# One pool of PSUM pairs for layer 0 and product 2, and block sums made inside the feature runs

## The chip, the cores and the metric

The kernel runs on one core of a Trainium2 chip. The core has TensorE (PE: matmuls, with its weight loads shown as PEld), VectorE (DVE), ScalarE (ACT), GpSimd (POOL) and SyncE (SP), whose queue starts most of the DMA transfers. Matmul results land in PSUM, which has eight banks of 512 fp32 values on each of 128 partitions; PE writes there, DVE and ACT read there. The metric is the device time of one execution in microseconds. Three executions of the kernel before gave 1660.17, 1660.75 and 1664.76 us, so its median is 1660.75.

## The reference, cut to what matters

The input is `x` (8 batches, 2048 nodes, 64 features) and an adjacency matrix `adj` (2048 x 2048). Four layers follow each other, each of the form `x = layernorm(x + layer(x))`, all in fp32.

```python
def _L0_gnn_ref(x, A, embedding, weight, bias):        # K = 3
    w = einsum('nd,dkio->nkio', embedding, weight)     # one weight matrix for every node
    b = einsum('nd,do->no', embedding, bias)
    As = [eye(N), A, 2.0 * (A @ A) - eye(N)]
    x_g = einsum('knm,bmc->bnkc', stack(As), x)
    return einsum('bnki,nkio->bno', x_g, w) + b
...
x = layernorm(x + L0(x, adj, embedding, weight, bias))
x = layernorm(x + L1(x, adj, net_params))      # z = relu((adj @ z) @ W), two times
x = layernorm(x + L2(x, adj, ...))             # x @ Wself + (adj @ x) @ Wneigh + bias
x = layernorm(x + L3(x, adj, adj, weight, bias))   # x, adj@x, adj@(adj@x) side by side, times weight, + bias
```

Each layer needs one or two products of `adj` with a 2048 x 512 matrix (8 batches of 64 features side by side). There are seven, one after another: the code's first stage makes product 0, and six calls of the function `product` make products 1 to 6. Layer 0 uses products 0 and 1, layer 1 uses 2 and 3, layer 2 uses 4, layer 3 uses 5 and 6.

## The kernel before

**A product of matrices with fewer multiplications.** `product` splits `adj` and the data into two by two quarters and uses seven products of quarters in place of eight (A11, S1, A12, S2, S4, S3, A22 in this order). Each of the seven is done by `inner`, which splits once more in the same manner: seven block products of 512 x 512, each one load of 1 MB of `adj` (or of sums of its blocks) and eight (in products 4 and 6, 32 smaller) matmul records on PE. `inner` first makes four block sums of its data, `t1` to `t4`, on DVE (`less`, L534). It then uses three PSUM banks a, b, c in the order `a+=`, `b+=`, `a+=`, `b+=`, `c+=`, `b+=`, `c+=` (L568 to L594). After the first block product ACT copies bank a to `p1` (L574), because the third accumulates onto it. In products 2 to 6 four of the seven inner products (`FORMED`) go instead through `fast_inner`, which splits twice more and uses seven banks after one another (L480 to L510); the sums of `adj` that it needs, the "forms", are made beforehand.

**Layer 0's feature step.** Whenever a block of product 1 (512 nodes x 2 batches, 16 blocks in all) is done, `hand_over` adds a job `feature0` to the pump. A job has four groups of nodes, and two halves of the embedding for each: a tile `y` of two PSUM banks, 12 matmul records. Of the first half (an odd tile) DVE takes eight readings (L1514, `xy += y * e`). Of the second half (an even tile) ACT takes eight (L1518, `s = y * e`), which POOL adds up in three steps (L1524) and onto `xy` (L1527). The job yields after each tile: these are its eight steps.

**The pump.** `Pump` holds jobs and, in `later`, normalizations that wait for a number of steps. `tick`, called at each step, counts these down; a normalization of a pair of blocks comes due three times: its square on ACT (L865), then the rest (the sum L872 and small steps on DVE, the root L881 on ACT, the scaling L893 on DVE), then its end. `run` works off whole jobs without the inner products between them. Beside them, after each step, it advances a list of side jobs at a given rate per step, and at its end it finishes them. Layer 0 has two runs: four jobs after S2 of product 1 (run 1, 32 steps, rate 1.25, side work: the forms of S1), and the other twelve at the start of product 2 (run 2, 96 steps, rate 0.97, side work: the forms of A12, S2 and S4). `make_forms` yields four times while its first tiles load and then once for each of 28 forms per quarter; 18 of the 28 are made by DVE and 10 by POOL (L289, L292), and each that is kept is stored by a transfer on SP's queue (L269).

**Order.** The framework schedules each engine's instructions at compile time, by when it thinks they are ready, and adds the semaphores. Instructions in `keep_in_program_order` stay behind everything written earlier for their engine: DVE's readings of `y`, the forms, POOL's adds, the first matmul of an odd `y` tile, the block sums of `inner` at the places in question, and the first seven loads of product 2. ACT's readings, `sq`, the root and the copy `p1` are not pinned.

**PSUM.** Before layer 0's second stage the banks belong to the pools `p_n` (`ps_n`) and `p_tn` (`ps_e`), four each. Then `p_mm` (two banks) serves the inner products, and `p_y` (three pairs, six banks) the `y` tiles. `to_late`, at the start of product 2, gives back `p_y` and allocates `p_mm2` (two banks, used in turn with `p_mm` from then on, see `bank`) and `p_z` (four banks).

**The run of the calls in `product`.** Product 1: A11, S1, A12, then a run of one job (a weight preparation), S2, run 1 (L788), S4, S3, A22. Product 2: run 2 (L697), then `to_late` and A11 (L744) with its block sums, S1 and the rest.

Of the kernel before, what the change touches and what calls it, by code (L numbers as in the profile page):

```python
# [9 lines left out]
F32 = mybir.dt.float32  # L10
AF = mybir.ActivationFunctionType
ALU = mybir.AluOpType
# [4 lines left out]
P = 128  # L17
EPS = 1e-5
GW = 512
# [38 lines left out]
class Pump:  # L58
# [32 lines left out]
                self.later.remove(job)  # L91

    def tick(self, idle=False):
        for job in list(self.later):

            job[0] -= 0.5 if idle and job[4] else 1
            if job[0] <= 0:
                job[0], job[4] = job[1], False
                if next(job[2], "done") == "done":
                    self.later.remove(job)  # L100

    def run(self, n=None, side=(), rate=1):

        side, owed = list(side), 0
        while self.jobs and n != 0:
            for _ in self.jobs[0]:
                self.tick()
                owed += rate
                while owed >= 1:
                    owed -= 1  # L110
                    if side and next(side[0], "done") == "done":
                        side.pop(0)
            self.jobs.pop(0)
            n = None if n is None else n - 1
        for job in side:
            for _ in job:
                pass
# [23 lines left out]
def kernel(  # L141
# [91 lines left out]

    loads = 0
    pieces = []
    banks = 0
    p_mm2 = None

    def load(q, s, forms=False):
        nonlocal loads  # L240
# [65 lines left out]
    def product(src, feature, between=None, rate=1, own=None, pin=False, runs=None, onto_slot=None, ends=False, fast=(), forms={}):  # L306
# [18 lines left out]
            return sums.tile([P, 4, GW], F32, tag="C", name="C", bufs=4)  # L325

        def bank(n):
            nonlocal banks
            banks += 1
            pool = p_mm if p_mm2 is None or banks % 2 else p_mm2  # L330
            return pool.tile([P, GW], F32, tag="mm", name=f"mm{n}")

        class InTile:

# [176 lines left out]
            if end is not None:  # L511
                end()

        def inner(q, b, finish, early=None, tail=None, next_sum=None, home=None, held=False):

            b11, b12, b21, b22 = (
                b[:, hm * TG : (hm + 1) * TG, ts(hc, 2 * F)] for hm in range(2) for hc in range(2)
            )  # L520

            places = [] if home is None else [tiled(home[:, k]) for k in range(4)]

            def new():
                if places:
                    return places.pop(0)
                return sums.tile([P, TG, 2 * F], F32, tag="t", name="t", bufs=TB)


            pin = tc.keep_in_program_order if places or pump.hold or held else lambda inst: inst  # L530

            def less(a, b):
                out = new()
                pin(nc.vector.tensor_tensor(out, a, b, ALU.subtract))  # L534
                return out

            t1 = less(b12, b11)
            t2 = less(b22, t1)
            t3 = less(b22, b12)
            t4 = less(b21, t2)  # L540
            if next_sum is not None and home is None:
                next_sum()

            def mul(ps, s, xb, start, stop=True):
                a = load(q, s)
                if onto_slot is not None:

                    for k in range(TG):
                        for m in range(TG):
                            if isinstance(ps, list):  # L550
                                to = ps[k // (TG - 1)][:, ts(k % (TG - 1), P)]
                                opens = k % (TG - 1) == 0
                            else:
                                to, opens = ps[:, ts(k, P)], k == 0
                            nc.tensor.matmul(  # L555
                                to, a[:, k, m, :], xb[:, m, :], start=(start and opens and m == 0),
                                stop=(m == TG - 1), skip_group_check=True,
                            )
                    pump.step(pump.rate)
                    return  # L560
                for m in range(TG):
                    nc.tensor.matmul(  # L562
                        ps, xb[:, m, :], a[:, :, m, :], start=(start and m == 0),
                        stop=(m == TG - 1), skip_group_check=True,
                    )
                pump.step(pump.rate)

            pa, pb = bank("a"), bank("b")  # L568
            mul(pa, 0, b11, True)
            if next_sum is not None and home is not None:  # L570

                next_sum()
            p1 = sums.tile([P, GW], F32, tag="p1", name="p1")
            nc.scalar.copy(p1, pa)  # L574
            if early is not None:
                early(2, p1)
            mul(pb, 5, t2, True)
            u2 = add(sums.tile([P, GW], F32, tag="u2", name="u2"), pb, p1)
            if early is not None:
                early(1, u2)  # L580
            mul(pa, 1, b21, False)
            finish(0, pa, None)
            mul(pb, 6, t3, False)
            u3 = add(sums.tile([P, GW], F32, tag="u3", name="u3"), pb, p1)
            if early is not None:
                early(3, u3)
            pc = bank("c")
            mul(pc, 4, t1, True)
            if tail is None:
                finish(3, pc, u3)  # L590
                mul(pb, 3, t4, False)
                finish(2, pb, p1)
                mul(pc, 7, b22, False)
                finish(1, pc, u2)  # L594
            else:
                parts = [p_z.tile([P, GW], F32, tag="z", name=f"mmd{h}") for h in range(2)]
                tail(pc, pb, parts, lambda: mul(pb, 3, t4, False), lambda: mul(parts, 7, b22, True))

        def fresh(c):
            def finish(blk, ps, plus):  # L600
                if plus is None:
                    nc.scalar.copy(c[:, blk, :], ps)
                else:
                    add(c[:, blk, :], ps, plus)
            return finish,

        def onto(c, base, give=None, then=None):

            def early(blk, plus):
                add(c[:, blk, :], base[:, blk, :], plus)  # L610
                if give is not None and onto_slot is not None:
                    add(tiled(c[:, blk, :]), place(*give, blk), tiled(c[:, blk, :]))

            def finish(blk, ps, plus):
                if give is not None and onto_slot is not None:
                    if plus is None:
                        add(place(*give, blk), place(*give, blk), tiled(base[:, blk, :]))
                    add(place(*give, blk), tiled(ps), place(*give, blk) if plus is None else tiled(c[:, blk, :]))
                else:
                    add(c[:, blk, :], ps, (base if plus is None else c)[:, blk, :])  # L620
                if give is not None:
                    hand_over(c, *give, blk)
                if then is not None:
                    then(blk)
            return finish, early
# [64 lines left out]
        give = onto_slot is not None  # L690
        waits = pump.hold and runs is None

        def side(q):
            return [make_forms(*forms[q])] if q in forms else []

        if waits:
            pump.run(None, side(A11), 0.97)  # L697
            pump.hold = False
        pump.pass_mark()

# [39 lines left out]
        if A11 in fast:  # L740
            next_sum()
            fast_inner(A11, b11, InTile(u), clear(u))
        else:
            inner(A11, b11, *fresh(u), home=home, next_sum=next_sum, held=waits)  # L744
        if pump.hold and not waits:
            pump.run()
            pump.hold = False
# [37 lines left out]
            fast_inner(S2, t2, InTile(u), None, join_all)  # L785
        else:
            inner(S2, t2, *onto(u, u, then=join))
        pump.run(runs.get(S2, 0), side(S2), 1.25)  # L788
        if S4 not in fast:
            inner(S4, b22, *onto(c, c, (0, 1)))  # L790
        elif give:
            fast_inner(S4, b22, InPlace(0, 1), spread(0, 1, c), hand_all(u, 0, 1))
        else:
            fast_inner(S4, b22, InTile(c), None, hand_all(c, 0, 1))
# [150 lines left out]
    if True:  # L945
# [487 lines left out]
            )  # L1433
            yield

        p_mm = ctx.enter_context(tc.tile_pool(name="p_mm", bufs=2, space=PSUM))
        if True:
            p_y = first.enter_context(tc.tile_pool(name="p_y", bufs=3, space=PSUM))
            l0y = first.enter_context(tc.tile_pool(name="l0y", bufs=1))

            def last_back():
# [93 lines left out]
    late = p_z = None  # L1535

    def to_late():
        nonlocal late, p_z, p_mm2, ring2, loads
        first.close()
        late = ctx.enter_context(tc.tile_pool(name="late", bufs=1))  # L1540
        ring2 = ctx.enter_context(tc.tile_pool(name="ring2", bufs=3))
        loads = 0
        p_mm2 = ctx.enter_context(tc.tile_pool(name="p_mm2", bufs=2, space=PSUM))
        p_z = ctx.enter_context(tc.tile_pool(name="p_z", bufs=4, space=PSUM))

    def pair_transposed(g, p, slot):
# [117 lines left out]
```

## Time and profile before

One execution was profiled. It took 1660.59 us; the span from its first to its last instruction is 1658.8 us.

| engine | busy, us | share of the span |
|---|---|---|
| PE | 1628.8 | 98% |
| PE weight loads | 1167.0 | 70% |
| DVE | 1128.8 | 68% |
| POOL | 572.1 | 34% |
| ACT | 308.6 | 19% |

The mean granted clock of PE is 0.996. Product 1 starts at 208.6 us, run 1 at 305.7, its S4 at 388.3, run 2 at 465.6, product 2's first matmul at 727.5.

How to read the lines below: in a list of groups or in the timeline a row names engine, line of the code, operation, output and inputs, and in brackets how long the engine sat idle before it and what ended that. A row of the waits reads "who <- for whom: total us, times, longest us". In the chain, a row is start, length and the work that held up the end. A row of a stretch (`392.00:401.00`) gives its length, the busy time and the number of instructions of PE, PEld, DVE, ACT and POOL, the granted clock of PE (1.00 is full), the share of the DMA engines and GB/s. Times are microseconds from the start of the span.

### The profile page before, as it was taken

What the parts mean: (1) busy time and instruction counts of PE and PEld (TensorE: products, weight loads), DVE (VectorE), ACT (ScalarE), POOL (GpSimd) and SP (SyncE); (2) the same over time, 40 slices, a digit from 0 to 9 for tenths busy, and PEclk for the clock granted to TensorE, in tenths of its full rate; (3) what the DMA queues carried; (4) which work ended last, traced back from release to release, by engine and by line L of the source; (5) the groups of instructions that cost most, each with busy time, mean ns of one, the idle gap of its engine ahead of it and who ended that gap; (6) DMA issues with size and microseconds to landing.
All of it is one profiled execution on the core that took longest, in us unless ns stands there. A gap on an engine that the chain in (4) does not pass through costs nothing.

```text
span 1658.8 us, 23256 instructions
## 1 busy us (share of the span) xinstructions
PE 1628.8 (98%) x8886; PEld 1167.0 (70%) x8886; DVE 1128.8 (68%) x1889; ACT 308.6 (19%) x870; POOL 572.1 (34%) x582
## 2 busy tenths in 40 slices
PE   9999999999999999989999999999999999999998
PEld 5998844444444444547875688579999688669998
DVE  5996795686458787755764378875689456644687
ACT  0210100243024344421111011221111012100111
POOL 1121100383037677763701451024522442025510
PEclk9999999999999999999999999999999999999999
DMA  8999999646843545369787877656888865678885
GB/s 312 358 389 375 347 334 323 232 149 238 304 159 117 201 137 185 105 234 345 274 288 259 286 279 254 227 211 236 292 295 298 293 247 199 251 249 282 305 308 176
DMA packets 101390, 429.47 MB, mean 259 GB/s; under 512 B 10752, under 2 KB 31616, under 8 KB 61856
## 3 DMA queue, kind: packets, MB, share of 16 engines
q1 hardware_dynamic: 87616, 380.34, 65.0%
q0 software_dynamic: 12016, 46.27, 7.3%
q8 instruction: 71, 1.16, 0.3%
q10 hardware_dynamic: 1648, 1.38, 0.3%
q14 instruction: 39, 0.32, 0.1%
HBM read 346.16 MB, written 81.79 MB: 258 GB/s over the span
## 4 chain that ended last, share of the span: by engine, by line
PE 90%; DVE 7%; issue 1%; DMA 0%; POOL 0%; ACT 0%; SPq 0%; DVEq 0%; POOLq 0%
PE y L1504 16%; PE mm L443 15%; PE mm L437 10%; PE mmb L562 10%; PE mmc L562 7%; PE mma L562 7%; PE ps_n L1285 6%; PE mmb L555 4%; PE ps_i L1199 3%; PE mmc L555 2%; PE mma L555 2%; PE z L1558 2%; DVE xy L1514 2%; PE z L1587 2%; PE ps_n L1239 2%
## 5 line engine op out<-in xcount | busy, mean ns | idle before, releaser
L1524 POOL TENSOR_TENSOR s<-s 128x512 f32<-128x512 f32 (+2 forms) x192 | 166.0, 864 | 274.5 <-ACT s L1518 264.1
L1514 DVE SCALAR_TENSOR_TENSOR xy<-y,e_sb,xy 128x128 f32<-128x128 f32 x512 | 179.3, 350 | 73.1 <-PE y L1504 57.2
L1518 ACT ACTIVATE s<-y,e_sb 128x128 f32<-128x128 f32 x512 | 139.3, 383 | 208.0 <-PE y L1504 192.3
L562 PE MATMUL mmb<-a,t 128*128 128x512 f32 x360 | 163.7, 598 | 3.0 <-DVE t L534 3.0
L1504 PE MATMUL y<-wn,xT 64*128 64x512 f32 x512 | 134.0, 593 | 7.2 <-DVE xy L1514 7.2
L443 PE MATMUL mm<-a,f 128*128 128x256 f32 x576 | 135.1, 380 | 0.7 <-POOL f L389 0.6
L1504 PE MATMUL y<-wn,tT 64*128 64x512 f32 x512 | 133.9, 593 | 0.0
L1504 PE MATMUL y<-wn,C 64*128 64x512 f32 x512 | 133.4, 591 | 0.0
L562 PEld LDWEIGHTS mmb<-a,t 128*128 128x128 f32 x360 | 67.8, 192 | 83.7 <-issue 78.9
L389 POOL TENSOR_TENSOR f<-T 128x512 f32<-128x512 f32 x20 | 26.5, 1340 | 275.5 <-PE mmb L562 124.7
L443 PEld LDWEIGHTS mm<-a,f 128*128 128x128 f32 x576 | 108.7, 190 | 17.3 <-POOL f L389 1.5
L1504 PEld LDWEIGHTS y<-wn,xT 64*128 64x128 f32 x512 | 52.4, 187 | 66.3 <-issue 64.8
L1504 PEld LDWEIGHTS y<-wn,C 64*128 64x128 f32 x512 | 53.5, 188 | 57.2 <-issue 57.2
L1504 PEld LDWEIGHTS y<-wn,tT 64*128 64x128 f32 x512 | 53.5, 188 | 57.0 <-issue 56.5
L437 PE MATMUL mm<-f,a 128*128 128x128 f32 x768 | 92.4, 275 | 0.0
L437 PEld LDWEIGHTS mm<-f,a 128*128 128x128 f32 x768 | 89.0, 192 | 0.1
L476 DVE TENSOR_TENSOR p<-p,mm 128x512 f32<-128x512 f32 x60 | 41.0, 684 | 61.3 <-PE mm L443 41.6
L318 DVE TENSOR_TENSOR u<-mmb,p 128x512 f32<-128x512 f32 x44 | 30.2, 686 | 68.8 <-PE mmb L562 59.4
L466 DVE TENSOR_TENSOR C<-C,mm 128x512 f32<-128x512 f32 x80 | 54.2, 683 | 29.5 <-PE mm L443 22.4
L562 PE MATMUL mma<-a,T 128*128 128x512 f32 x160 | 72.1, 594 | 0.0
L1007 POOL DMA_DIRECT2D comb<-si x29 | 22.0, 758 | 138.2 <-DVE si L998 138.2
L555 PE MATMUL mmb<-t,a 128*128 128x128 f32 x576 | 67.3, 275 | 0.0
(241 smaller groups left out, 3030.4 us busy)
## 6 DMA issues: line engine op xcount, KB each, us to landing
a<-comb SPq DMA_DIRECT2D x127, 1024.0 KB, 5.0
a<-form SPq DMA_DIRECT2D x120, 1024.0 KB, 4.8
a<-in_blocks SPq DMA_DIRECT2D x43, 1024.0 KB, 4.9
comb<-si POOLq DMA_DIRECT2D x29, 1024.0 KB, 10.7
form<-form SPq DMA_DIRECT2D x88, 256.0 KB, 2.7
a<-in_slices SPq DMA_DIRECT2D x15, 1024.0 KB, 11.3
comb<-so POOLq DMA_DIRECT2D x15, 1024.0 KB, 13.3
a<-form SPq DMA_DIRECT2D x20, 512.0 KB, 4.9
```

Of the source, the lines that this page charges most:

```text
L437: nc.tensor.matmul(ps[:, ts(2 * h + j, P)], a[:, j, m, :], x[:, m, :], start=(start and h == j == m == 0), stop=(m == 1), skip_group_check ...
L443: nc.tensor.matmul(ps[:, ts(h, GW // 2)], x[:, m, :], a[:, :, m, :], start=(start and h == m == 0), stop=(m == 1), skip_group_check=True,)
L466: nc.vector.tensor_tensor(out, out, view(v), op)
L476: nc.vector.tensor_tensor(e, e, halves(ps), op)
L555: nc.tensor.matmul(to, a[:, k, m, :], xb[:, m, :], start=(start and opens and m == 0), stop=(m == TG - 1), skip_group_check=True,)
L562: nc.tensor.matmul(ps, xb[:, m, :], a[:, :, m, :], start=(start and m == 0), stop=(m == TG - 1), skip_group_check=True,)
L1199: nc.tensor.matmul(ps, x[:, m // 2, m % 2], s[n](m), start=(start and m == 0), stop=(m == TG - 1), skip_group_check=True,)
L1285: nc.tensor.matmul(ps[:, ts(p, GW // 2)], b(k, p), a(k // TG, k % TG), start=(start and p == k == 0), stop=(k == NT // 2 - 1), skip_group_ ...
L1504: mm = nc.tensor.matmul(y[:, b, :], terms[n][half, ts(k, P)], wn[half, n, h * DH : (h + 1) * DH, :], start=(n == 0), stop=(n == 2),)
L1514: tc.keep_in_program_order(nc.vector.scalar_tensor_tensor(acc, y[:, :, ts(d, F)], e, acc, ALU.mult, ALU.add))
L1518: nc.scalar.activation(s[:, d], y[:, :, ts(d, F)], AF.Copy, scale=e)
L1524: nc.gpsimd.tensor_tensor(s[:, :n], s[:, :n], s[:, n : 2 * n], ALU.add)
```

## The change

Three things change together.

1. **PSUM.** In layer 0, `p_y` has four pairs instead of three, and all eight banks. The inner products of product 1 take their banks from it: a and b are the two banks of one pair, c is one bank of the next (its other bank stays unused; `spare` is cleared at each inner product). From product 2 on there is a single pool `p_mm` of four banks, allocated in `to_late` after `p_y` is given back, in place of `p_mm` and `p_mm2` in turn.
2. **Side work.** `tick` says whether a normalization came due. In `run`, such a step counts one side step less. The rate of run 1 becomes 1.28 (it was 1.25) and that of run 2 1.08 (0.97).
3. **Block sums.** `prepare_sums` is a new side job behind `make_forms` in both runs: it makes the four block sums of the inner product that follows the run (S4 of product 1, A11 of product 2), with the same instructions on DVE. That `inner` gets them as `ready` and leaves out its own.

```diff
     def tick(self, idle=False):
+        busy = False
         for job in list(self.later):
             job[0] -= 0.5 if idle and job[4] else 1
             if job[0] <= 0:
                 job[0], job[4] = job[1], False
+                busy = True
                 if next(job[2], "done") == "done":
                     self.later.remove(job)
+        return busy
...
             for _ in self.jobs[0]:
-                self.tick()
-                owed += rate
+                owed += rate - self.tick()
                 while owed >= 1:
                     owed -= 1
                     if side and next(side[0], "done") == "done":
...
         def bank(n):
-            nonlocal banks
-            banks += 1
-            pool = p_mm if p_mm2 is None or banks % 2 else p_mm2
-            return pool.tile([P, GW], F32, tag="mm", name=f"mm{n}")
+            if p_mm is not None:
+                return p_mm.tile([P, GW], F32, tag="mm", name=f"mm{n}")
+            if not spare:
+                pair = p_y.tile([P, 2, GW], F32, tag="y", name=f"mm{n}")
+                spare.extend([pair[:, 0], pair[:, 1]])
+            return spare.pop(0)
...
-            t1 = less(b12, b11)
-            t2 = less(b22, t1)
-            t3 = less(b22, b12)
-            t4 = less(b21, t2)
+            if ready:
+                t1, t2, t3, t4 = ready
+            else:
+                t1 = less(b12, b11)
+                t2 = less(b22, t1)
+                t3 = less(b22, b12)
+                t4 = less(b21, t2)
...
+            spare.clear()
             pa, pb = bank("a"), bank("b")
...
-        def side(q):
-            return [make_forms(*forms[q])] if q in forms else []
+        ready = []
+
+        def prepare_sums(b):
+            c11, c12, c21, c22 = (
+                b[:, hm * TG : (hm + 1) * TG, ts(hc, 2 * F)] for hm in range(2) for hc in range(2)
+            )
+            for x, y in ((c12, c11), (c22, 0), (c22, c12), (c21, 1)):
+                t = sums.tile([P, TG, 2 * F], F32, tag="t", name="t", bufs=TB)
+                y = ready[y] if isinstance(y, int) else y
+                tc.keep_in_program_order(nc.vector.tensor_tensor(t, x, y, ALU.subtract))
+                ready.append(t)
+                yield
+
+        def side(q, b=None):
+            return [make_forms(*forms[q]), prepare_sums(b)] if q in forms else []

         if waits:
-            pump.run(None, side(A11), 0.97)
+            pump.run(None, side(A11, b11), 1.08)
...
-            inner(A11, b11, *fresh(u), home=home, next_sum=next_sum, held=waits)
+            inner(A11, b11, *fresh(u), home=home, next_sum=next_sum, held=waits, ready=ready)
...
-        pump.run(runs.get(S2, 0), side(S2), 1.25)
+        pump.run(runs.get(S2, 0), side(S2, b22), 1.28)
         if S4 not in fast:
-            inner(S4, b22, *onto(c, c, (0, 1)))
+            inner(S4, b22, *onto(c, c, (0, 1)), ready=ready)
...
-        p_mm = ctx.enter_context(tc.tile_pool(name="p_mm", bufs=2, space=PSUM))
         if True:
-            p_y = first.enter_context(tc.tile_pool(name="p_y", bufs=3, space=PSUM))
+            p_y = first.enter_context(tc.tile_pool(name="p_y", bufs=4, space=PSUM))
...
-        p_mm2 = ctx.enter_context(tc.tile_pool(name="p_mm2", bufs=2, space=PSUM))
+        p_mm = ctx.enter_context(tc.tile_pool(name="p_mm", bufs=4, space=PSUM))
         p_z = ctx.enter_context(tc.tile_pool(name="p_z", bufs=4, space=PSUM))
```

More of the change, by code (lines that the diff above doesn't have):

```diff
@@ L235 @@
     pieces = []
-    banks = 0
-    p_mm2 = None
+    spare = []
+    p_mm = p_y = None
     def load(q, s, forms=False):
@@ L512, in fast_inner, with inner @@
                 end()
-        def inner(q, b, finish, early=None, tail=None, next_sum=None, home=None, held=False):
+        def inner(q, b, finish, early=None, tail=None, next_sum=None, home=None, held=False, ready=None):
             b11, b12, b21, b22 = (
@@ L1537, in to_late @@
     def to_late():
-        nonlocal late, p_z, p_mm2, ring2, loads
+        nonlocal late, p_z, p_mm, ring2, loads
         first.close()
```

## The prediction

> **What bounds the kernel now.** I read the page's busy times first, then the waits of TensorE (PE) alone, then the chain in order of time around each, and last the other engines in those few microseconds. The busy times:
>
> ```profile
> PE 1628.8 (98%) x8886; PEld 1167.0 (70%) x8886; DVE 1128.8 (68%) x1889; ACT 308.6 (19%) x870; POOL 572.1 (34%) x582
> ```
>
> PE's waits between 300 and 740 us (who for whom: us in total, times, longest):
>
> ```profile
> PE y L1504 <- DVE xy L1514: 7.2, 4, 3.7
> PE mma L562 <- ACT s L1518: 4.6, 1, 4.6
> PE mmb L562 <- DVE t L534: 3.0, 1, 3.0
> ```
>
> PE is the bound, so only its gaps can be won. It idles 1658.8 - 1628.8 = 30.0 us, and these six waits, all in layer 0, are 14.8 us of it. The chain (start, length) and the granted clock from 392 to 401 us (0.81) show that they have a second price:
>
> ```profile
> 395.00 5.40 PE mmb L562 x8
> ...
> 559.64 7.13 PE y L1504 x24
> ...
> 647.44 10.59 PE y L1504 x48
> ...
> 727.54 5.29 PE mma L562 x8
> ```
>
> ```profile
> 392.00:401.00 9.00, 6.00 (x10) 2.60 (x11) 6.16 (x7) 2.31 (x6) 4.15 (x4) 0.81 0.32 117
> ```
>
> Eight `mm` records normally take 3.43 us, and 24 `y` records 24 x 0.2145 = 5.15. Behind the waits of 3.04, 3.69 and 4.55 us they take 5.40, 7.13 and 5.29: each long wait costs 1.97, 1.98 or 1.86 us more. Behind the wait of 2.02 us (before 647.44) 48 records take 10.59, where 48 x 0.2145 is 10.30: no such price.
>
> **Part 1, run 1 and its end.** Run 1 is four feature jobs, 32 steps of one `y` tile (12 records, 2.575 us); VectorE (DVE) reads the odd tiles, ScalarE (ACT) the even ones. The new rate gives 1.28 x 32 = 40.96 side steps, less 2 for the normalization (steps 28 and 32): 38. They are 4 landing, 28 forms, 1 end, 4 block sums, 1 end; the sums fall at steps 27, 29, 29 and 30. DVE pays at least 4 x 0.68 us; it idles 2.10 us per two tiles there, so the sums fit, or push its last reading by up to 1 us. The wait of 3.04 us goes. What is late next stands on ACT and GpSimd (POOL):
>
> ```profile
> 397.28 1.06 ACT L865 ACTIVATE sq<-xy 128x1024 f32<-128x1024 f32 x1 [4.50 <-POOL xy L1527]
> 398.24 0.57 ACT L574 COPY p<-mma 128x512 f32<-128x512 f32 x1
> ```
>
> ```profile
> 392.86 3.52 POOL L1524 TENSOR_TENSOR s<-s 128x512 f32<-128x512 f32 x3 [4.17 <-ACT s L1518]
> ```
>
> The third product adds onto bank a, so it needs the copy `p` (L574); ACT has `sq` (L865) queued ahead of it, and `sq` waits for POOL's adds. Before, `p` ended at 398.8 and the third product began at 400.40: covered. Now products one and two end at 388.25 + 2 x 3.43 = 395.1, and behind the third stands all of PE's queue. POOL's adds take 2.61 + 0.46 us where DVE forms no sums beside them (its rows inside the run), so they end at 392.86 + 3.07 = 395.9, `sq` at 397.0, `p` at 397.6. With 0.3 us for DVE's push the third product starts at 397.9: 2.5 us earlier than 400.40, behind a new wait of 2.8 us. Does this wait halve the clock? 2.02 did not and 3.04 did; 2.8 is nearer to 3.04, so I charge 1.97. Net gain 0.5. Ends: a gain of 3.04 + 1.97 = 5.0, if ACT copies first; a loss of 0.2, with the full push (400.40 - 398.6 - 1.97).
>
> [...]
>
> **Part 2, the waits inside run 2** (12 jobs, 96 steps). DVE around the longest:
>
> ```profile
> 545.71 3.05 DVE L1514 SCALAR_TENSOR_TENSOR xy<-y,e_sb,xy 128x128 f32<-128x128 f32 x8 [2.10 <-PE y L1504]
> 548.67 1.71 DVE L292 TENSOR_TENSOR form<-form,a 128x512 f32<-128x512 f32 x1
> 550.30 1.21 DVE L872 TENSOR_REDUCE ss<-sq 128x16 f32<-128x1024 f32 x1
> ...
> 554.78 1.75 DVE L292 TENSOR_TENSOR form<-form 128x512 f32<-128x512 f32 x1
> 556.45 5.62 DVE L1514 SCALAR_TENSOR_TENSOR xy<-y,e_sb,xy 128x128 f32<-128x128 f32 x15
> ```
>
> From one tile's reading to the next takes 10.7 us instead of 5.15: two forms and a normalization (550.30 to 554.78). PE runs out of its three pairs at 559.64 - 3.69 = 555.95 and gets one when the first eight of the last row are done. The fourth pair lets PE do one more tile, to 558.5. The form at 554.78 leaves this step, which the normalization takes up, so the pair is free at 559.6 - 1.75 = 557.9: no wait. The other three (2.02, 1.15 and 0.33) are each below the 2.575 us that a pair adds. The forms put off are made at other steps: per two tiles DVE then has 3.05 + 2.16 x 18/28 x 1.0 = 4.4 of 5.15 us, so its lag shrinks between normalizations, and POOL 3.07 + 2.16 x 10/28 x 1.4 = 4.2. Gain 7.2 + 1.98 = 9.2. Ends: 9.2, and 2.0 (the waits stay, shortened below the clock's limit).
>
> [...]
>
> **Part 3, the end of run 2.** Normalization acts at 13 steps (4, 28, 32, 36, 40, 44, 60, 64, 68, 72, 76, 92, 96), so there are 1.08 x 96 - 13 = 90 side steps, where 0.97 x 96 gave 93. The last form, number 88, moves from step 91 to 93; one block sum (0.68 us) falls at step 95, three behind the run, where product 2 made them anyway. The first stands on DVE ahead of the normalization; ACT runs that one's root before its last eight readings (725.16 and 725.28 us), and product 2's first matmul waits for these. So it comes 0.7 us later, at 728.2, and the 4.55 + 1.86 us stay, since the new pool lies where `p_y` lay. In SP's queue the loads of product 2 stand behind the last form's store:
>
> ```profile
> 715.90 0.42 SPq L251 DMA_DIRECT2D a<-in_blocks  x1
> ```
>
> Two steps are 5.15 us: this load leaves at 721.0 and, landing in 6.0 us, is there at 727.0, covered by 1.2 us. Ends: a loss of 4.7, if POOL gets to that form one pair of tiles later (721.0 + 5.15 + 6.0 = 732.2 against 727.54); a gain of 4.1, if ACT's readings go ahead of the root (done at 725.2 instead of 727.45, and no 1.86).
>
> **Part 4, the first matmul of product 1.** Its bank lay over those of `ps_n`, and it followed PE's last `ps_e` at once (208.55). `p_y` now spans all eight banks; if a pool waits for all that lay there, as at 727.54, it waits for DVE's reading of `ps_e`:
>
> ```profile
> 208.75 0.75 DVE L1301 TENSOR_TENSOR hT<-ps_e,u 128x256 f32<-128x256 f32 x2 [4.17 <-PE ps_e L1285]
> ```
>
> Done at 209.5: a loss of 1.0; the other end is none. In layer 0 each inner product takes two of the four pairs and the next the other two: no wait.
>
> **Part 5, the later products.** Two pools of two banks, used in turn, become one of four; in rotation they are the same. Nothing. Ends: a gain of 5.4 (all of PE's 3.3 + 1.5 + 0.6 us of waits there for DVE's L463, L476 and L466), and the loss of rival C.
>
> **Sum:** -0.5 - 9.2 + 0.7 + 1.0 = -8.0 us. The profiled execution took 1660.59 (span 1658.8 and 1.8 around it), 0.2 below the median 1660.75. So 1652.7; its own range is 1648 (part 1 or 3 at its better end) to 1657 (both at their worse).
>
> **Rivals.** A, DVE stays late: with PE unstalled its lag adds up from one normalization to the next, part 2 brings its lower end 2.0, and all comes to 1660, no change. For it: DVE is busy 203 of 263 us in run 2. Against it: 4.4 of 5.15. B, the ends of both runs come free, because ACT's queue comes out in another order: -5.0 - 9.2 - 4.1 + 1.0 = -17.3, 1643. For it: only order puts `sq` and the root ahead. Against it: nothing upstream of them moves by more than 1 us. C, slower: in the later products the one pool hands out its banks so that PE waits. The longest such wait of before is 1.6 us, and there are 20 fast inner products: 5 waits eat the 8.0, 9 make the kernel slower by 0.3%, one in each of the 20 gives 1685. Against it: the banks come free in the order in which they were taken.
>
> **How the numbers follow.** 0.3% is 5.0 us, about what a measurement can tell from no change. Forecast 0.63, A 0.14, B 0.12, C 0.11. A tenth of the forecast's chance lies above 1655.8, as does nearly all of A; so faster is 0.57 + 0.12 + 0.02 = 0.71. C and a dearer end of run 2 give slower 0.10, the rest is same, 0.19. The range takes in A and half of B, and leaves out C's dear half: 1643 to 1661.
>
> **What would show it.** No PE wait for `xy` L1514 in run 2; none for `t`, but one for ACT's L574 near 396, of 2 to 3 us; one for ACT's `s` at run 2's end, of 5 us; one of 1 us near 209; PE's waits behind layer 0 unchanged. It is wrong if `y` still waits for DVE, or if new waits for banks show in the later products.

## The result, and the profile after

The changed kernel takes 1667.97 us (median of 10 runs), the kernel before 1661.68 us in 10 runs. The ratio is 1.0040, with a 95% interval of 1.0027 to 1.0052: slower by 0.4%, where 1652.7 us were forecast. The profiled execution took 1666.12 us, its span is 1664.3. The page of the changed kernel, PE's row of busy times:

```profile
PE 1630.2 (98%) x8886; PEld 1154.2 (69%) x8886; DVE 1122.3 (67%) x1889; ACT 308.6 (19%) x870; POOL 574.1 (34%) x582
```

PE does the same 8886 instructions and idles 34.1 us instead of 30.0. The starts of the stages, from the timelines of PE, say where. The span grew by 5.5 us, and that is the sum of the differences:

| stage | before, us | after, us | difference |
|---|---|---|---|
| up to product 1's first matmul | 208.55 | 209.80 | +1.25 |
| product 1: A11, S1, A12, S2 | 97.10 | 106.54 | +9.44 |
| run 1 | 82.60 | 82.60 | 0.00 |
| product 1: S4, S3, A22 | 77.31 | 84.57 | +7.26 |
| run 2, up to product 2's first matmul | 261.98 | 250.12 | -11.86 |
| all that follows | 931.26 | 930.67 | -0.59 |

Run 2 won more than was forecast. Product 1 lost 16.7 us, for which the forecast had next to nothing. PE's waits in the changed kernel, first in the stretch up to run 1 (200 to 320 us), then around S4 to A22 (380 to 484 us):

```profile
PE mma L569 <- DVE u L320: 3.3, 4, 0.9
PE mma L569 <- ACT p L582: 2.2, 3, 0.7
PE mmc L569 <- DMA a<-comb: 1.1, 1, 1.1
PE mma L569 <- DVE hT L1322: 1.1, 1, 1.1
```

```profile
PE mma L569 <- ACT p L582: 7.1, 3, 5.7
PE mma L569 <- DVE u L320: 0.8, 1, 0.8
PE mmc L569 <- DMA a<-comb: 0.4, 1, 0.4
```

None of these stood before; the one for `hT` is the 1.0 us that part 4 of the prediction charged. Both banks of a pair now carry the name `mma`, because a and b are cut from one tile. One inner product on PE, after:

```profile
237.50 3.60 PE L569 MATMUL mma<-a,T 128*128 128x512 f32 x8
241.81 3.70 PE L569 MATMUL mma<-a,t 128*128 128x512 f32 x8 [0.72 <-ACT p L582]
246.36 3.70 PE L569 MATMUL mma<-a,T 128*128 128x512 f32 x8 [0.85 <-DVE u L320]
249.90 1.02 PE L569 MATMUL mmc<-a,t 128*128 128x512 f32 x2
250.76 3.68 PE L569 MATMUL mma<-a,t 128*128 128x512 f32 x8
254.28 2.74 PE L569 MATMUL mmc<-a,t 128*128 128x512 f32 x6
...
263.72 3.60 PE L569 MATMUL mma<-a,xy 128*128 128x512 f32 x8
```

The second block product goes into bank b, and waits for ACT's copy of bank a. The third goes into bank a, and waits for DVE's reading of bank b (`u`). The fifth, into bank c, is cut in two: 2 records stand ahead of the fourth product and 6 behind it. From one inner product's start to the next's 26.2 us go by instead of 7 x 3.43 = 24.0.

At the end of run 1 this wait meets the copy `p` that stands behind `sq`, on PE and on ACT of the changed kernel:

```profile
398.94 3.70 PE L569 MATMUL mma<-a,xy 128*128 128x512 f32 x8
408.29 5.64 PE L569 MATMUL mma<-a,t 128*128 128x512 f32 x8 [5.65 <-ACT p L582]
```

```profile
406.71 1.06 ACT L886 ACTIVATE sq<-xy 128x1024 f32<-128x1024 f32 x1 [3.24 <-POOL xy L1547]
407.67 0.57 ACT L582 COPY p<-mma 128x512 f32<-128x512 f32 x1
```

The chain behind `p` is the forecast one. But not the third product stands there; already the second does, 5.65 us.

In run 2 PE waits for DVE no more. Its 96 tiles before, and after (the columns are length, busy time of PE, PEld, DVE, ACT and POOL, granted clock, DMA share, GB/s):

```profile
465.60:722.99 257.39, 250.21 (x1153) 122.29 (x1152) 198.85 (x466) 107.89 (x385) 183.15 (x218) 0.99 0.44 147
```

```profile
483.50:731.00 247.50, 247.49 (x1153) 111.49 (x1152) 195.40 (x466) 107.86 (x385) 186.63 (x218) 1.00 0.45 148
```

They take 247.5 us, and 96 x 2.575 is 247.2. At the run's end PE waits 2.65 us, not for ACT but for the first load of product 2. It left at 727.81, behind the last form's store, 3.2 us before PE was through with its last `y`:

```profile
733.63 5.09 PE L569 MATMUL mma<-a,xy 128*128 128x512 f32 x8 [2.65 <-DMA a<-in_blocks]
```

```profile
727.81 0.42 SPq L253 DMA_DIRECT2D a<-in_blocks  x1
```

### The profile page after: what moved, and what is told of

Same layout as the page of the kernel before. It is cut to its first block, busy times and chain, and to the rows that moved or that the text cites. A ratio compares the mean times of both kernels' runs of the same rounds, so it can differ in the third digit from the quotient of the medians.

```text
span 1664.3 us, 23257 instructions
## 1 busy us (share of the span) xinstructions
PE 1630.2 (98%) x8886; PEld 1154.2 (69%) x8886; DVE 1122.3 (67%) x1889; ACT 308.6 (19%) x870; POOL 574.1 (34%) x582
## 4 chain that ended last, share of the span: by engine, by line
PE 93%; DVE 4%; DMA 1%; issue 1%; ACT 0%; POOL 0%; ACTq 0%; SPq 0%; DVEq 0%; POOLq 0%
PE y L1524 19%; PE mm L447 15%; PE mma L569 10%; PE mm L441 10%; PE mmc L569 7%; PE ps_n L1306 6%; PE mmb L569 6%; PE mmb L562 4%; PE ps_i L1220 3%; PE z L1578 2%; PE mmc L562 2%; PE mma L562 2%; PE z L1607 2%; PE ps_n L1260 1%; PE pt L1569 1%
## 5 line engine op out<-in xcount | busy, mean ns | idle before, releaser
L569 PE MATMUL mmb<-a,t 128*128 128x512 f32 x216 | 97.1, 592 | 0.0
L1524 PEld LDWEIGHTS y<-wn,C 64*128 64x128 f32 x512 | 49.6, 187 | 60.3 <-issue 60.3
L1524 PEld LDWEIGHTS y<-wn,tT 64*128 64x128 f32 x512 | 49.5, 187 | 60.4 <-issue 60.1
L569 PE MATMUL mma<-a,t 128*128 128x512 f32 x144 | 67.9, 616 | 9.3 <-ACT p L582 9.3
L569 PEld LDWEIGHTS mmb<-a,t 128*128 128x128 f32 x216 | 40.0, 190 | 45.0 <-issue 45.0
```

The source lines that it names most:

```text
L569: nc.tensor.matmul(ps, xb[:, m, :], a[:, :, m, :], start=(start and m == 0), stop=(m == TG - 1), skip_group_check=True,)
L1524: mm = nc.tensor.matmul(y[:, b, :], terms[n][half, ts(k, P)], wn[half, n, h * DH : (h + 1) * DH, :], start=(n == 0), stop=(n == 2),)
```

## The experiments

**Theory 1:** to the framework that places the semaphores, the two halves of a pair are one tile. So a matmul into b waits for the reading of a, and the reverse, though no matmul into the one needs what is read from the other. **The rival:** it is the sharing itself; inner products and `y` tiles draw on one pool, and pairs come free late. The first four runs answer this, and split the change into its PSUM part and its side work. All ratios are against the kernel before on the same chip (1660.58 us, 9 runs, for these four).

**1. Each product bank from a pair of its own.** The pool, the four pairs and the side work of the change stay; three pairs instead of two go into one inner product.

```diff
-            if not spare:
-                pair = p_y.tile([P, 2, GW], F32, tag="y", name=f"mm{n}")
-                spare.extend([pair[:, 0], pair[:, 1]])
-            return spare.pop(0)
+            return p_y.tile([P, 2, GW], F32, tag="y", name=f"mm{n}")[:, 0]
```

> The changed kernel, but each bank of product 1's inner products is the first bank of a pair of its own, so that banks a and b are no longer two halves of one tile. Three of the four pairs serve one inner product. Theory 1 (the framework sees the pair as one tile: a matmul into bank b waits for ACT's or DVE's reading of bank a, and PE's order is rearranged around that): the first three inner products take 97.0 us again instead of 106.6, those from S4 to A22 some 75 to 77 instead of 84.7, and the time is 1647 to 1650 us; at the end of run 1 PE waits 2 to 3 us for the copy p, at the third block product instead of 5.7 us at the second. Rival (sharing one pool with the y tiles is what makes PE wait, since pairs come free late): with three pairs of four per inner product the waits stay or grow, 1666 us or more.

Measured: 1649.74 us, ratio 0.9934 (0.9920 to 0.9949). The four inner products from A11 on take 97.18 us, those from S4 76.47. PE's waits between 200 and 740 us are only these:

```profile
PE mma L566 <- DVE nw L905: 3.9, 1, 3.9
PE mma L566 <- ACT p L579: 2.2, 1, 2.2
PE mma L566 <- DVE hT L1319: 1.1, 1, 1.1
```

The same stretch of one inner product as above, with PE's plain order a, b, a, b back:

```profile
234.26 3.60 PE L566 MATMUL mma<-a,T 128*128 128x512 f32 x8
237.70 3.60 PE L566 MATMUL mmb<-a,t 128*128 128x512 f32 x8
241.13 3.60 PE L566 MATMUL mma<-a,T 128*128 128x512 f32 x8
244.56 3.60 PE L566 MATMUL mmb<-a,t 128*128 128x512 f32 x8
```

The pool is shared as in the changed kernel, and even more pairs are in use, so the rival falls. The waits for DMA in product 1 are gone as well. Product 1 alone is 17.5 us shorter than in the changed kernel (106.54 - 97.18 and 84.57 - 76.47); the two spans differ by 16.4 us, since among other things PE waits 1.3 us longer at the end of run 2 here. The first row of the waits names DVE's `nw`, which only ended at about the same moment; the load of product 2 left at 709.82 and landed 7.0 us later, 0.1 us before PE started at 716.91.

**2. The PSUM part alone, as in the change.** Shared pairs, old side work.

```diff
-                owed += rate - self.tick()
+                self.tick()
+                owed += rate
...
-            return [make_forms(*forms[q]), prepare_sums(b)] if q in forms else []
+            return [make_forms(*forms[q])] if q in forms else []
...
-            pump.run(None, side(A11, b11), 1.08)
+            pump.run(None, side(A11), 0.97)
...
-        pump.run(runs.get(S2, 0), side(S2, b22), 1.28)
+        pump.run(runs.get(S2, 0), side(S2), 1.25)
```

> Only the PSUM part of the change: shared pool of four pairs, a and b in one pair; side work at the old rates 1.25 and 0.97, normalizations not counted, block sums made by the inner product itself. Theory 1: product 1 loses as in the changed kernel, 1.1 at its start, 9.6 in its first three inner products, and takes 84 to 85 us from S4 to A22; the fourth pair alone removes run 2's waits (9.2 us with their clock price); the end of run 2 waits 4.5 us for ACT as before. Together some 1668 to 1671 us. If the skipped side work is what removed the waits in run 2: two or three of them stay, 1672 to 1676.

Measured: 1671.84 us, ratio 1.0069 (1.0054 to 1.0084). That is 0.8 us above the first range and just under the second, so the time alone does not decide; the waits do. Of run 2's waits for DVE one of 1.1 us is left, not two or three, so the fourth pair does most of that work. Product 1 loses as in the change (106.19 and 86.35 us). From S4 on it takes longer than the expected 84 to 85; the wait for `p` at the end of run 1 is 6.9 us here instead of 5.65.

**3. The side work alone.** The pools of before, the rest of the change.

```diff
-            if p_mm is not None:
-                return p_mm.tile([P, GW], F32, tag="mm", name=f"mm{n}")
...
+            pool = p_mm if p_mm2 is None or banks % 2 else p_mm2
+            return pool.tile([P, GW], F32, tag="mm", name=f"mm{n}")
...
-            p_y = first.enter_context(tc.tile_pool(name="p_y", bufs=4, space=PSUM))
+            p_y = first.enter_context(tc.tile_pool(name="p_y", bufs=3, space=PSUM))
```

> Only the side work: the pools of before (two banks for the inner products, three pairs for y, from product 2 on two pools in turn), with the new rates, the normalizations counted and the block sums made in the runs. Theory 1: product 1 keeps its 97.0 us; at the end of run 1 PE waits 2 to 3 us for the copy p instead of 3.0 for t; in run 2 waits for DVE of 4 to 6 us in sum stay, none long enough for the clock; the end of run 2 waits for the first load (2 to 3 us) instead of 4.6 for ACT. Time 1652 to 1657 us. Rival (the side work does the harm, by moving forms, stores and loads): slower than before, 1664 or more.

Measured: 1654.89 us, ratio 0.9963 (0.9950 to 0.9975). The side work does no harm. PE's waits from 200 to 740 us:

```profile
PE y L1524 <- DVE xy L1534: 4.8, 3, 2.0
PE mma L568 <- ACT rs L901: 3.0, 1, 3.0
PE mma L568 <- ACT p L581: 2.2, 1, 2.2
```

In run 2 4.8 us of waits stay and none exceeds 2.0, as expected. The second row is named after the root `rs` on ACT, but it is the load that PE waits for, as expected too:

```profile
714.47 0.42 SPq L254 DMA_DIRECT2D a<-in_blocks  x1
717.78 2.18 ACT L1538 ACTIVATE s<-y,e_sb 128x128 f32<-128x128 f32 x8 [2.97 <-PE y L1524]
```

The load landed 6.1 us after it left, at 720.6, and the matmul started at 720.70. ACT's last readings had ended at 719.96. The root ended at 720.64, but the matmul does not need it: in experiment 5 the root starts at 711.81, after the matmul at 711.76.

**4. Pairs of their own, with the old side work.** The edits of 1 and 2 together.

> Pairs of their own for the banks of product 1, and the side work of before. Theory 1: 1.0 us lost at the start of product 1; run 2 without its waits for DVE, since the fourth pair (2.6 us of lead) covers 2.0, 1.2 and 0.3 and most of 3.7: 8 to 9 us gained; the ends of both runs as before (3.0 for t and 4.5 for ACT, each with the clock price). Time 1653 to 1656 us. If the fourth pair does not suffice without the skipped steps: waits of 2 us or more stay in run 2 and the time is above 1657.

Measured: 1653.70 us, ratio 0.9958 (0.9943 to 0.9973). One wait of 1.1 us for DVE stays in run 2, and the ends of both runs are as before (3.3 for `t`, 4.6 for ACT). The four runs and the two kernels make a table (us):

| | old side work | new side work |
|---|---|---|
| pools of before | 1660.6 to 1661.7 | 1654.9 |
| shared pairs, a and b in one | 1671.8 | 1668.0 |
| shared pairs, one bank of each used | 1653.7 | 1649.7 |

Putting a and b into one pair costs 18 us in either column. The other parts gain: the new side work 4 to 6 us in each row, the fourth pair with separate pairs 5 to 7 us in each column.

**5. The copy before the square.** What is left at the end of run 1 shows in the kernel of experiment 1: a wait of 2.21 us for `p` and eight records in 5.40 us. Here, on top of experiment 1, `sq` is pinned on ACT behind what is written before it.

```diff
-                self.pin(nc.scalar.activation(self.sq[:, t0:t1], self.v[:, t0:t1], AF.Square))
+                tc.keep_in_program_order(nc.scalar.activation(self.sq[:, t0:t1], self.v[:, t0:t1], AF.Square))
```

> As own_pair (1649.7 us), with the square sq of the normalizations pinned behind what is written before it on ACT, so that at the end of run 1 the copy p of bank a stands ahead of sq. If the wait of 2.21 us for p, and the 5.40 instead of 3.43 us of the eight records behind it, come from that order in ACT's queue: both go, 2.2 + 2.0 = 4.2 us, 1645 to 1646 us. If p is late for another reason (ACT's last readings, the root): no more than 1 us.

Measured: 1644.28 us, ratio 0.9900 (0.9884 to 0.9917), with the kernel before at 1661.58 in these last three runs. S4 to A22 take 72.30 us instead of 76.47: 4.2 us, as expected. The order of ACT's queue was the cause. The median lies 0.7 us under the expected range. In the profile the end of run 2 came out shorter as well: PE waits 2.81 us for the load there instead of 3.91, and no half clock follows (the granted clock is 1.00 from 707.50 to 714.30 us).

**6. An earlier last form.** On top of experiment 1, the rate of run 2 is 1.12 instead of 1.08.

```diff
-            pump.run(None, side(A11, b11), 1.08)
+            pump.run(None, side(A11, b11), 1.12)
```

> As own_pair, with the rate of run 2 at 1.12 instead of 1.08: the last form falls at step 89 instead of 93, all four block sums inside the run, and the first load of product 2 leaves some 10 us earlier (it landed 7.0 us after its issue at 709.82 and PE began at 716.91). The load no longer holds PE. The framework then puts the root ahead of ACT's last eight readings, as in the kernel before: PE waits some 4.5 us for these instead of 3.9 us for the load, and the time stays at 1649 to 1651 us. If the load were not what held PE in own_pair: the same wait as there, 3.9 us, with the load landed long before. In run 2 no waits for DVE in either case.

Measured: 1651.10 us, ratio 0.9937 (0.9922 to 0.9951). The load leaves at 700.70 and is no longer waited for. Instead PE waits 4.6 us for ACT, which runs the root ahead of its last readings again. Alone this gains nothing: the next wait in line takes its place.

**7. Both, and the root pinned.** As 6, with the edit of 5, and the root pinned in the same way.

```diff
-            self.pin(nc.scalar.activation(self.rs, self.rs, AF.Sqrt))
+            tc.keep_in_program_order(nc.scalar.activation(self.rs, self.rs, AF.Sqrt))
```

> As own_rate, with sq and the root both pinned behind what is written before them on ACT: the copy p ahead of sq at the end of run 1, ACT's last readings ahead of the root at the end of run 2. Theory 1: no wait for p (4.2 us with its clock price), and at the end of run 2 PE waits about 2.3 us for ACT's last eight readings, not for the load (3.9): 1.6 us less, and perhaps 1.9 us of clock. Together 1642 to 1645 us. If what is gained in one queue comes back in another (POOL's adds, DVE's sums): 1646 us or more.

Measured: 1642.37 us, ratio 0.9885 (0.9871 to 0.9900): faster than the kernel before by 1.15%, and faster than the changed one by 25.6 us. Two waits of PE are left between 200 and 740 us:

```profile
PE mma L566 <- ACT rs L899: 2.4, 1, 2.4
PE mma L566 <- DVE hT L1319: 1.1, 1, 1.1
```

The first is named after the root, which ends at 711.65. But PE does not need the root (see experiment 3); ACT's last readings end at 711.55 and the matmul starts at 711.65, so it is these that PE waits for.

## The prediction, point by point

**Part 4 is the step that failed**, in its last sentence: "In layer 0 each inner product takes two of the four pairs and the next the other two: no wait." It looked at when a pair comes free for the next inner product, and not at what happens inside one, where a and b are read and written in turn. That term was put at 0 and measured 16.7 us in the changed kernel (9.44 + 7.26, with what came out better at S4 already in it). Experiment 1 shows that it is the shared tile: with banks of their own the same sum comes out at 1649.7 us against the 1652.7 forecast. None of the three rivals had this. C, the slower one, looked for waits on banks in the later products; these took 930.67 us against 931.26. Of the two signs of being wrong that the prediction named, neither showed; the loss lay in product 1, where it had named none. The other term of part 4, 1.0 us for DVE's reading of `ps_e`, measured 1.05.

**Part 1** had the chain right (POOL's adds, `sq`, `p`) and said that products one and two end before it binds. With a shared pair the second product waits for it too: 5.65 us instead of 2.8. With separate banks (experiment 1) the wait is 2.21 us at the third product, and the clock price 5.40 - 3.43 = 1.97 comes with it as charged. That charge was luck: it went by the length of the wait, and 2.21 is nearer to the 2.02 that cost nothing than to 3.04. The last section has waits of 2.81 and 3.04 us that cost nothing either; what decided, no run shows. The net gain there, 77.31 - 76.47 = 0.8 us, was forecast as 0.5 (reckoned from the 400.40 of the chain; PE's timeline has that product start at 400.23, which makes the forecast 0.4). Experiment 5 shows the better end: S4 to A22 came down by 5.0 us against before, the very 5.0 named.

**Part 2** was right: all waits for DVE in run 2 went. The 96 tiles gained 257.4 - 247.5 = 9.9 us against 9.2 forecast. Experiments 2, 3 and 4 divide the causes: with the fourth pair alone one wait of 1.1 us stays, which is the longest of before less a tile (3.69 - 2.575); with the skipped forms alone three waits of 4.8 us in sum. The working asked for both only in the longest wait. Rival A, a lag of DVE that adds up, did not show. In experiment 4 the fourth pair brought 6.9 us (1653.7 against 1660.6).

**Part 3** missed the order of ACT's queue. It left the root ahead of the last readings and charged 0.7 us on that. In the changed kernel the framework put the readings first, which was the better end of the working, and the load of product 2 became the limit: it left 3.2 us before PE was through and landed in 5.7. So PE started 2.65 us behind its last `y` instead of 4.55, a gain of 1.9 where a loss of 0.7 was forecast; a clock price came with it as before (5.09 us for eight records). The load's own delay was seen, and put too high: it was reckoned to leave 1.9 us before PE was through. The order on ACT went with the side work. With that of before (the kernel before, experiments 2 and 4) the root stands first; with that of the change (the changed kernel, experiments 1, 3 and 5) the readings do; at the rate of 1.12 (experiment 6) the root does again. Why the framework's schedule turns there, no run shows.

**Part 5** held: PE's waits behind layer 0 are almost the same (3.3, 1.5, 1.2 and 1.0 us; before 3.3, 1.5, 1.2, 0.6 and 0.6).

The forecast put 0.10 on slower, and the measured 1667.97 lies above its range, which ended at 1661. All the parts that were priced came within 3 us of their price (part 1 in experiment 1, where a and b are apart); the term put at nothing cost 16.7 us, twice the 8.0 that they were to bring.

## What to carry to other kernels

When a change puts two buffers into one tile, list who reads and who writes each half, and when: here the framework made the writer of one half wait for the readers of the other, and a matmul order that alternates between the halves paid for it in every inner product. Buffers that a user takes two at a time as one tile do not work as two. And once a wait is gone, look at the order of the queue of whoever comes next (`sq` ahead of `p`, the root ahead of the readings): here pinning one instruction was worth 5.5 us (experiments 1 and 5) and pinning two 8.7 us (6 and 7), as much as the fourth pair.

## What the runs showed of the hardware

The price of a wait in clock does not follow from the wait's length alone. A wait of 2.21 us (experiment 1, at 396.2 us) was followed by a stretch at half clock, 0.50 from 399.40 to 402.80 us; one of 2.81 us (experiment 5, at 709.0) and one of 3.04 us (experiment 3, at 717.7) were not. In the kernel before another wait of 3.04 us, for `t`, was followed by half clock:

| kernel | wait, us | records behind it | granted clock, in the stretch (us) |
|---|---|---|---|
| before, `y` | 2.02 | 48 in 10.59 us | 1.00, 647.40 to 654.30 |
| experiment 5, load | 2.81 | 8 in 3.67 us | 1.00, 710.90 to 714.30 |
| experiment 3, load | 3.04 | 8 in 3.67 us | 1.00, 719.60 to 726.40 |
| experiment 1, `p` | 2.21 | 8 in 5.40 us | 0.50, 399.40 to 402.80 |
| changed kernel, load | 2.65 | 8 in 5.09 us | 0.50, 733.10 to 736.50 |
| before, `t` | 3.04 | 8 in 5.40 us | 0.50, 396.30 to 399.70 |

Nor is the price itself the same behind equal waits. At the end of run 2 three kernels wait 4.55 us for ACT; the eight records behind took 5.29 us in the kernel before, 6.13 in experiment 4 and 6.35 in experiment 6. Two stretches of experiment 1 in a row, the one with the wait and the one behind it (the clock is the number 0.50 behind POOL's):

```profile
396.00:399.40 3.40, 1.19 (x4) 0.52 (x4) 1.02 (x2) 1.53 (x2) 0.71 (x2) 1.00 0.86 318
399.40:402.80 3.40, 3.40 (x6) 1.32 (x5) 2.88 (x7) 0.22 (x1) 0.00 (x0) 0.50 0.26 108
```

and the same of experiment 5, whose wait is longer, from 708.95 to 711.76 us:

```profile
707.50:710.90 3.40, 1.45 (x8) 0.39 (x4) 3.22 (x8) 1.82 (x8) 1.86 (x4) 1.00 0.90 316
710.90:714.30 3.40, 2.54 (x6) 1.25 (x7) 2.94 (x7) 0.57 (x3) 2.81 (x3) 1.00 1.01 419
```

What decides whether the clock is halved, no run shows. The ten runs of the changed kernel differ in their mean granted clock too: 1664.19 us at 0.998, six runs from 1666.12 to 1668.38 at 0.996, three from 1670.29 to 1672.13 at 0.994. Which waits were followed by half clock in them, only the trace of the profiled one shows.
